# Weights loaded in runs of 128 columns, and four steps of a product moved, in a four-layer attention kernel

## The chip, the cores and the metric

The kernel runs on one core of a Trainium2 chip. A core has five engines that run side by side, each with its own queue of instructions: TensorE (PE in the profile; its weight loads are PEld) multiplies matrices, VectorE (DVE) and ScalarE (ACT) do elementwise work, GpSimd (POOL) does a little more of it, and SyncE (SP) issues DMA transfers. Sixteen DMA engines move the data between HBM and the core's memory (SBUF). The metric is device time in microseconds, the median of several executions. TensorE, VectorE and ScalarE hand data to each other through SBUF and through PSUM, the banks that matrix products are written to.

## What is computed

The input x has 8 images of 512 channels by 1024 positions. Four layers follow each other; what matters here is the first two, and of them the weights.

```python
# layer 0, per image b
f = relu(batchnorm(Wf @ x)); g = relu(batchnorm(Wg @ x)); h = Wh @ x      # 64 channels each
z = f.T @ g;  x = Wv @ (h @ (z / largest_singular_value(z)).T) + x
# layer 1
n = group_norm(x)
q = wq @ n + bq;  k = wk @ n + bk;  v = wv @ n + bv
x = x + wp @ (v @ softmax(q.T @ k / sqrt(512)).T) + bp
# layer 2: attention again with other weights; layer 3: a convolution with signs of weights and inputs
```

The statistics of layer 0's batchnorm run over all images, so all of x is read once before anything else can end.

The kernel doesn't compute q and k apart. With u = (wk.T wq) n the scores are u.T n, up to terms that the softmax drops, and with wo = wp wv the output projection is folded in too. So it makes two products of weights at the start, `wu` from q and k and `wo` from v and p, and two bias vectors: `bu`, the sum over the rows of wk weighted by bq, and `bo`, the sum over wp's columns weighted by bv (plus bp). Each of these is a sum over one common index of 512. Its order is free, so long as both factors have it in the same order.

## The kernel before, in words

**First passes (L1361 to L1413).** For b = 0 to 7, `load_x(b)` fetches an image in four DMAs of 512 KB (L141, the first image in five), one for each 128 channels, and TensorE multiplies it with the weights of f, g and h (L1376); for the last two images h is left for later. The tile `xt` has two buffers: the load of image b waits until pass b-2 has read its buffer for the last time. ScalarE and VectorE copy the products out and take statistics (L1395 to L1404). The last two images stay in their buffers.

**Loads between the images.** SP's queue is in program order. After the four x loads of b = 2, 3 and 4 it issues the loads of wq, wk and wv (`load_blocks`, L1334 to L1343), 16 DMAs of 64 KB each: a DMA fills 32 partitions, and its source is read in runs of 32 neighbouring columns. After v's come `load_rows` (L210 to L214): the bias row bg_row, the vector bvc (bv of layer 1) and Wv of layer 0 twice. Then come x of b = 5 and 6, the weights z, tpg and p (`load_w`, L156), and x of b = 7. A DMA instruction takes one of eight semaphores in turn, and waits until the DMA that had it before, eight DMAs earlier, has landed.

**Transposes.** In the product of weights, the common index has to lie on the partitions. The weights arrive with the other index there. `natural` (L1345 to L1350) turns each by four VectorE transposes of 32x32 blocks: with w on partitions 32 q to 32 q + 31 loaded from columns of group q, the transposed columns come to lie on those partitions. Which column is on which partition follows from the loads alone.

**Second part (L1551 to L1627).** TensorE's order is written out by hand: a generator `filler` yields after each small piece of independent work, and the main thread of work, which has dependent steps on other engines, takes so many steps of it (`next(todo)`) after each of its own. `filler` loads p, makes wu (`product`, L1420), the late h, the Gram matrices, the biases (`biases`, L1443 to L1468), and last wo, again by `product`: 16 matmuls of 512 columns, with a copy by ScalarE after each 8. The main thread is the chain for the largest singular value (`first_chain`) and then the entry of the first image into layer 1 (`entering(0)`, which runs `enter`, L421 to L467): the two products for the image's weights (L301), four visits with matmuls (L431) and VectorE work (L440 to L445), a mean (L452), a variance (L459), and small steps on VectorE and GpSimd that end in scale and bias. The list in L1622 says how many filler steps go behind each of the seven. Then the normalized h is made (L482), which the first product of u (L407, through `make_u`) waits for.

For the other engines a scheduler chooses the order; the memset of `ones2` (L1632), for instance, is one that it moves.

Of the kernel before, what the change touches and what calls it, by code (L numbers as in the profile page):

```python
# [8 lines left out]
F32 = mybir.dt.float32  # L9
# [7 lines left out]
P = 128  # L17
B = 8
C = 512
N = 1024  # L20
CC = C // P
# [4 lines left out]
MID = 64  # L26
# [34 lines left out]
COL = {n: 4 * i for i, n in enumerate(VEC512)}  # L61
# [9 lines left out]
QUAD = 32  # L71
# [16 lines left out]
def kernel(  # L88
# [17 lines left out]
    nc = tc.nc  # L106
    mm = nc.tensor.matmul

    const = ctx.enter_context(tc.tile_pool(name="const", bufs=1))
# [15 lines left out]
    def bank():  # L125
        return psum["bank"].tile([P, HF], F32, tag="bank", name="bank")
# [20 lines left out]
    def side(i):  # L147

        return slice(i * MID, (i + 1) * MID)


    sbw = {}

    def load_w(name, src, shape, pool=wpool, eng=nc.sync, tag=None):
        t = pool.tile(shape, F32, tag=tag or name, name=name)
        eng.dma_start(out=t, in_=src)  # L156
        sbw[name] = t
        return t
# [4 lines left out]
    a1 = early.enter_context(tc.tile_pool(name="a1", bufs=1))  # L163
# [38 lines left out]
    bg_row = const.tile([P, P], F32, tag="bg_row", name="bg_row")  # L202

    bvc = const.tile([P, CC], F32, tag="bvc", name="bvc")
    bhc = const.tile([P, 1], F32, tag="bhc", name="bhc")
    wv2 = const.tile([P, C], F32, tag="wv2", name="wv2")
    for i in range(2):
# [1 line left out]

    def load_rows():  # L210
        nc.sync.dma_start(out=bg_row, in_=rows[MID + C :].partition_broadcast(P))
        nc.sync.dma_start(out=bvc, in_=rows[MID : MID + C].rearrange("(cc p) -> p cc", p=P))
        for i in range(2):
            nc.sync.dma_start(out=wv2[side(i), :], in_=w_v0)  # L214

# [10 lines left out]
    def vec(name):  # L226
        return ct[:, COL[name] : COL[name] + CC]
# [1094 lines left out]
    def scale_z():  # L1322

        rep = a1.tile([P, CC, P], F32, tag="absw", name="rep")
        nc.vector.tensor_copy(rep, inv2.unsqueeze(2).to_broadcast([P, CC, P]))
        ps = bank()
        for oc in range(CC):
            mm(out=ps[:, bass.ts(oc, P)], lhsT=rep[:, oc, :], rhs=ident, start=True, stop=True)
        nc.vector.tensor_tensor(sbw["z"], sbw["z"], ps, ALU.mult)


    nat = {}

    def load_blocks(name, src, tag):  # L1334

        t = sbw[name] = a1.tile([P, 4, GROUPS, QUAD], F32, tag=tag, name="blocks_" + name)
        of = src.rearrange("(r a) c o -> r a (c o)", a=QUAD)
        for q in range(4):
            for r in range(4):
                nc.sync.dma_start(  # L1340
                    out=t[bass.ts(q, QUAD), r],
                    in_=of[r].rearrange("a (m w) -> a m w", w=P)[:, :, bass.ts(q, QUAD)],
                )  # L1343

    def natural(name, tag):  # L1345
# [16 lines left out]
    for b in range(B):  # L1362
# [3 lines left out]
        if b in (2, 3, 4):  # L1366
            load_blocks(*((("q", w_q, "q"), ("k", w_k, "k"), ("v", w_v, "v"))[b - 2]))
        if b == 4:
            load_rows()
# [45 lines left out]
    def product(lt, rhs, dst, vector):  # L1415
        for i in range(CC // 2):
            ps = wide()
            for k in range(2):
                for oc in range(CC):
                    one = mm(  # L1420
                        out=ps[:, half(k)],
                        lhsT=lt[:, oc, bass.ts(2 * i + k, P)],
                        rhs=rhs[:, oc, :],
                        start=oc == 0,
                        stop=oc == CC - 1,
                    )
                    if i + k + oc == 0:
                        tc.keep_in_program_order(one)
                    if k == 0 or oc < CC - 1:
                        yield  # L1430
            to = dst[:, 2 * i : 2 * i + 2, :].rearrange("p o c -> p (o c)")
            if i % 2 and vector:
                nc.vector.tensor_copy(to, ps)
            else:
                nc.scalar.copy(to, ps)
            yield

    def biases():

        part = a1.tile([P, 2, C], F32, tag="absw", name="part")
        for j, (w, v) in enumerate(((nat["k"], vec("L1_conv_bq")), (sbw["p"], bvc))):  # L1443
            t = part[:, j, :]
            for k in range(CC):
                if k == 0:
                    nc.vector.tensor_scalar(t, w[:, 0, :], v[:, 0:1], None, ALU.mult)
                else:
                    nc.vector.scalar_tensor_tensor(
                        t, w[:, k, :], v[:, k : k + 1], t, ALU.mult, ALU.add  # L1450
                    )
                yield False
        for j, dst in enumerate((bu, bo)):
            ps = bank()
            for i in range(CC):
                mm(
                    out=ps[:, i : i + 1],
                    lhsT=part[:, j, bass.ts(i, P)],
                    rhs=ones1,
                    start=True,  # L1460
                    stop=True,
                )
            if dst is bu:
                nc.vector.tensor_copy(bu, ps[:, 0:CC])
            else:
                nc.vector.tensor_tensor(bo, ps[:, 0:CC], vec("L1_conv_bp"), ALU.add)
            yield True
        nc.vector.tensor_tensor(bvo, bo, vec("L0_conv_bv"), ALU.add)  # L1468
# [82 lines left out]
    def filler():  # L1551

        load_w("p", w_p, [P, CC, C], a1, tag="v")
        yield from product(nat["q"], nat["k"], wu, True)
        for b in order[:2]:
            yield from late_h(b)
        yield from gram(jl, 2, ht_pair[jl], gtl)
        scale_z()  # L1560
        yield
        between = biases()
        sums = sums_u()
        for j in rest:
            for _ in grams(j):
                next(sums, None)
                yield
                if next(between, None):
                    yield
        yield from product(nat["v"], sbw["p"], wo, False)  # L1570

    todo = filler()
    with tc.manual_schedule(engines={mybir.EngineType.PE}):
        mv = a1.tile([P, 2, 2], F32, tag="mv", name="mv")
        mean = a1.tile([P, 2], F32, tag="mean", name="mean")
        dev = a1.tile([P, 2], F32, tag="dev", name="dev")
        for i in range(2):
            nc.vector.bn_aggr(mv[:, i, :], st[:, i, :, :])
        for _ in range(3):
            next(todo)  # L1580
        ps = bank()
        mm(out=ps[:, 0:2], lhsT=fold, rhs=mv[:, :, 0], start=True, stop=True)
        nc.vector.tensor_copy(mean, ps[:, 0:2])
        nc.vector.tensor_tensor(dev, mv[:, :, 0], mean, ALU.subtract)
        nc.vector.tensor_tensor(dev, dev, dev, ALU.mult)
        nc.vector.tensor_tensor(dev, dev, mv[:, :, 1], ALU.add)
        next(todo)
        ps = bank()
        mm(out=ps[:, 0:2], lhsT=fold, rhs=dev, start=True, stop=True)
        sc0 = rsqrt_eps(a1, ps[:, 0:2], 2, "r0")  # L1590
        bi0 = a1.tile([P, 2], F32, tag="bi0", name="bi0")
        m0 = a1.tile([P, 2], F32, tag="m0", name="m0")
        c0 = COL["L0_conv_bf"]
        bias, gamma, beta = (ct[:, c0 + 2 * i : c0 + 2 * i + 2] for i in range(3))
        nc.vector.tensor_tensor(sc0, sc0, gamma, ALU.mult)
        nc.vector.tensor_tensor(m0, mean, bias, ALU.add)
        nc.vector.tensor_tensor(bi0, bias, m0, ALU.subtract)
        nc.vector.tensor_tensor(bi0, bi0, sc0, ALU.mult)
        nc.vector.tensor_tensor(bi0, bi0, beta, ALU.add)
        jl = order[0] // 2  # L1600
        for i in range(2):
            for k in range(2):
                relu(2 * jl + k, i)
        for _ in range(5):
            next(todo)
        for ftl, gtl in turned_pair(jl):
            pass
        for i, t in ((0, ftl), (1, gtl)):
            for _ in gram(jl, i, t, t):
                next(todo)  # L1610

        relus = iter([(2 * j + k, i) for j in rest for i in range(2) for k in range(2)])

        steps = entering(0)
        for k, _ in enumerate(first_chain(jl)):

            for _ in range(4 if k == 3 * NSTEP + 3 else 2 if k % 3 == 1 or k == 0 else 1):
                next(todo, None)
            for args in (next(relus, None),):
                if args:  # L1620
                    relu(*args)
        for n in (2, 2, 2, 2, 4, 3, 6):  # L1622
            next(steps)
            for _ in range(n):
                next(todo, None)
        for _ in todo:
            pass  # L1627
# [194 lines left out]
```

## Time and profile before

| | |
|---|---|
| median of 3 runs | 1891.7 us (1891.26 to 1892.12) |
| the profiled execution's own time | 1891.29 us |
| its span, first to last instruction | 1889.5 us |
| TensorE busy | 1856.3 us, 98% |
| VectorE busy | 1122.5 us, 59% |
| ScalarE busy | 541.7 us, 29% |
| GpSimd busy | 121.8 us, 6% |
| the first passes over x, TensorE | 4.31 to 102.4 us |
| the first product of u begins | 191.11 us |
| DMA packets | 50114, of them 28848 under 512 B |

The span is what the profile shows, and the 1.8 us that the execution's time has more lie around it. A single precision matmul of 512 columns stands in the trace as two records. In a timeline each row is a run of like instructions: its start in us, its length, engine, line, operation, tiles, how many, and in brackets how long the engine sat idle before it, and what it waited for. Times in rows of SP (SPq) are those in which SP works at issuing a DMA, not those of the transfer. The chain of work that ended last is followed back from the last instruction of the program through whatever released each step.

### The profile page before, as it was taken

How to read it: one execution, taken by the hardware profiler on the slowest of the kernel's cores; microseconds unless marked ns; L12 is line 12 of the kernel's file. 1: busy time of each engine (PE TensorE's matmuls, PEld its weight loads, DVE VectorE, ACT ScalarE, POOL GpSimd, SP SyncE). 2: the span in 40 equal slices, each digit the busy share in tenths (PEclk: the TensorE clock that was granted, in tenths of full speed). 3: DMA queues.
4: the chain of work that ended last, by engine and by line, in shares of the span. 5: the costliest groups of instructions: out<-in, count | busy, mean ns of one | idle time of the engine just before them, and what ended most of it. 6: DMA issues, size and time to landing. Idle time of an engine off the chain costs nothing.

```text
span 1889.5 us, 16517 instructions
## 1 busy us (share of the span) xinstructions
PE 1856.3 (98%) x6196; PEld 949.7 (50%) x6196; DVE 1122.5 (59%) x2083; ACT 541.7 (29%) x882; POOL 121.8 (6%) x109
## 2 busy tenths in 40 slices
PE   8799999999999999999999999999999999999997
PEld 3246456544645456544645455544645455544653
DVE  3246686467774676467774676357653766355547
ACT  2032221145203521234203522144202521244114
POOL 1000000100020000200020001100020001100011
PEclk9999999999999999999999999999999999999999
DMA  8810000002000110002000110002000200000001
GB/s 247 259 57 7 1 6 12 1 12 89 18 1 1 53 54 12 1 12 89 18 0 1 62 44 12 1 30 71 12 0 12 89 12 1 1 34 23 12 0 47
DMA packets 50114, 66.52 MB, mean 35 GB/s; under 512 B 28848, under 2 KB 30060, under 8 KB 49772
## 3 DMA queue, kind: packets, MB, share of 16 engines
q1 hardware_dynamic: 49100, 64.96, 10.2%
q8 instruction: 51, 0.84, 0.2%
q10 hardware_dynamic: 864, 0.43, 0.1%
q14 instruction: 35, 0.29, 0.1%
q0 software_dynamic: 64, 0.00, 0.0%
HBM read 46.44 MB, written 18.94 MB: 35 GB/s over the span
## 4 chain that ended last, share of the span: by engine, by line
PE 93%; SPq 3%; DVE 2%; ACT 1%; DMA 1%; issue 0%; POOL 0%; DVEq 0%; ACTq 0%
PE bank L407 46%; PE bank L585 20%; PE bank L834 6%; PE bank L987 5%; PE bank L686 3%; PE bank L703 3%; SPq L1340 2%; PE bank L1376 2%; PE bank L431 2%; PE bank L726 1%; PE wide L1420 1%; PE bank L1478 1%; PE bank L1055 1%; PE bank L857 0%; PE quad L1268 0%
## 5 line engine op out<-in xcount | busy, mean ns | idle before, releaser
L585 PE MATMUL bank<-e,vt 128*128 128x512 f32 x768 | 336.2, 594 | 0.0
L585 PEld LDWEIGHTS bank<-e,vt 128*128 128x128 f32 x768 | 144.6, 190 | 172.1 <-issue 167.6
L407 PE MATMUL bank<-ut,h 128*128 128x512 f32 x384 | 178.9, 598 | 0.0
L407 PEld LDWEIGHTS bank<-ut,h 128*128 128x128 f32 x384 | 71.4, 190 | 94.5 <-issue 92.9
L407 PE MATMUL bank<-us,hs 128*128 128x512 f32 x256 | 115.6, 593 | 0.0
L834 PE MATMUL bank<-tpg 128*128 128x512 f32 x256 | 115.4, 596 | 0.0
L987 PE MATMUL bank<-e,tpg 128*128 128x512 f32 x256 | 114.7, 595 | 0.0
L358 DVE TENSOR_TENSOR e<-bank,e 128x512 f32<-128x512 f32 x96 | 66.2, 689 | 60.8 <-PE bank L407 50.6
L841 ACT ACTIVATE e<-bank 128x512 f32<-128x512 f32 x128 | 76.3, 597 | 67.0 <-PE bank L834 67.0
L407 PE MATMUL bank<-h,wu 128*128 128x512 f32 x192 | 91.7, 610 | 3.5 <-DVE h L482 3.5
L352 ACT COPY e<-bank 128x512 f32<-128x512 f32 x96 | 56.0, 584 | 118.9 <-PE bank L407 118.5
L407 PE MATMUL bank<-wo,h 128*128 128x256 f32 x384 | 89.9, 384 | 0.0
L238 POOL TENSOR_TENSOR r_r<-r_v,minus_half 128x4 f32<-128x4 f32 (+1 forms) x11 | 10.9, 988 | 1057.9 <-DVE r_v L237 1052.0
L987 PEld LDWEIGHTS bank<-e,tpg 128*128 128x128 f32 x256 | 48.2, 190 | 60.3 <-issue 59.9
L407 PEld LDWEIGHTS bank<-wo,h 128*128 128x128 f32 x384 | 71.5, 190 | 12.5 <-issue 3.8
L407 PEld LDWEIGHTS bank<-us,hs 128*128 128x128 f32 x256 | 48.5, 190 | 57.3 <-issue 54.4
L1376 PE MATMUL bank<-xt,fg 128*64 128x512 f32 x256 | 61.8, 627 | 15.7 <-DMA xt<-in_x 11.3
L846 DVE TENSOR_TENSOR esum<-esum,e 128x1024 f32<-128x1024 f32 x48 | 58.8, 1225 | 30.2 <-ACT e L841 29.9
L834 PEld LDWEIGHTS bank<-tpg 128*128 128x128 f32 x256 | 47.7, 191 | 54.9 <-issue 52.3
L714 ACT ACTIVATE sg<-xt,rb 128x512 f16<-128x512 f32 x64 | 44.2, 716 | 107.7 <-DVE xt L705 104.8
L358 DVE TENSOR_TENSOR vt<-bank,vt 128x512 f32<-128x512 f32 x48 | 33.2, 691 | 66.4 <-PE bank L407 65.6
L352 ACT COPY vt<-bank 128x512 f32<-128x512 f32 x64 | 37.3, 583 | 121.4 <-PE bank L407 121.3
(361 smaller groups left out, 2885.5 us busy)
## 6 DMA issues: line engine op xcount, KB each, us to landing
xt<-in_x SPq DMA_DIRECT2D x55, 512.0 KB
out<-both SPq DMA_DIRECT2D x63, 256.0 KB
rfull<-r_dram SPq DMA_DIRECT2D x15, 512.0 KB
f_dram<-f SPq DMA_DIRECT2D x8, 256.0 KB
fb<-f_dram SPq DMA_DIRECT2D x8, 256.0 KB
w<-in_w SPq DMA_DIRECT2D x1, 1024.0 KB
blocks_q<-in_w_q SPq DMA_DIRECT2D x16, 64.0 KB
blocks_k<-in_w_k SPq DMA_DIRECT2D x16, 64.0 KB
```

The source lines that it names most:

```text
L352: nc.scalar.copy(dst, ps)
L358: nc.vector.tensor_tensor(dst, ps, u, ALU.add)
L407: mm(out=ps[:, q * w : (q + 1) * w], lhsT=lt(ka, kb, q, k), rhs=rhs(ka, kb, q, k), start=first and q == 0 and k == 0, stop=last and k == 1 ...
L585: mm(out=ps, lhsT=a[:, t, bass.ts(r_, P)], rhs=e[t], start=first and t == 0, stop=last and t == NTH - 1, skip_group_check=True,)
L686: mm(out=ps[:, i, :], lhsT=xt[:, cc, bass.ts(4 * h + i, P)], rhs=sbw["tpg"][:, cc, 2 * P : 3 * P], start=cc == 0, stop=cc == CC - 1,)
L703: mm(out=ps, lhsT=sbw["z"][:, bass.ts(oc, P)], rhs=att, start=True, stop=True)
L714: nc.scalar.activation(sg[:, cc, :], xt[:, cc, half(h)], AF.Sign, bias=rb3[:, cc : cc + 1])
L834: mm(out=ps, lhsT=pt[:, 0, bass.ts(t, P)], rhs=tt[:, 0, half(h)], start=True, stop=True,)
L841: nc.scalar.activation(e[:, half(h)], ps, AF.Exp, scale=float(P) ** -0.5)
L846: nc.vector.tensor_tensor(esum, esum, e, ALU.add)
L987: mm(out=banks[h], lhsT=gt[:, t, :], rhs=es[t][:, half(h)], start=t == 0, stop=t == NT - 1,)
L1376: mm(out=banks[i][side(h), :], lhsT=w0[i][:, cc, :], rhs=xt[:, cc, half(h)], start=cc == 0, stop=cc == CC - 1,)
```

## The change

Four things change.

1. `load_blocks` reads runs of 128 neighbouring columns where it read runs of 32. The number of DMAs (16 for each weight), their size (64 KB) and their 32 partitions stay; a group q of 32 partitions now gets columns 128 q to 128 q + 127 of each row chunk, where it got columns 32 q to 32 q + 31 out of each 128. The transposes are not touched. Through them the common index comes in another order on partitions and chunks.
2. p has to have its rows in that same order, and is loaded in four DMAs of 256 KB, one for each group of 32 partitions, where it was one of 1 MB with 128 partitions.
3. The two vectors that weight the rows in `biases` need that order too. bvc is loaded in four DMAs of 32 partitions by 4 elements, where it was one of 128 by 4. bq was read from the tile of all columns that is there anyway; a tile of its own, bqc, is now loaded by four more DMAs. These are all on SP's queue, in `load_rows`.
4. The list of filler steps is (2, 2, 2, 2, 3, 2, 4) where it was (2, 2, 2, 2, 4, 3, 6).

```diff
@@ -202,6 +202,7 @@
     bvc = const.tile([P, CC], F32, tag="bvc", name="bvc")
+    bqc = const.tile([P, CC], F32, tag="bqc", name="bqc")
@@ -209,7 +210,11 @@
     def load_rows():
         nc.sync.dma_start(out=bg_row, in_=rows[MID + C :].partition_broadcast(P))
-        nc.sync.dma_start(out=bvc, in_=rows[MID : MID + C].rearrange("(cc p) -> p cc", p=P))
+        rv = rows[MID : MID + C].rearrange("(q m b) -> q b m", q=4, b=QUAD)
+        rq = cols.rearrange("(m b) n -> n b m", b=QUAD)
+        for q in range(4):
+            nc.sync.dma_start(out=bvc[bass.ts(q, QUAD), :], in_=rv[q])
+            nc.sync.dma_start(out=bqc[bass.ts(q, QUAD), :], in_=rq[COL["L1_conv_bq"] + q])
         for i in range(2):
             nc.sync.dma_start(out=wv2[side(i), :], in_=w_v0)
@@ -1334,12 +1339,12 @@
         t = sbw[name] = a1.tile([P, 4, GROUPS, QUAD], F32, tag=tag, name="blocks_" + name)
-        of = src.rearrange("(r a) c o -> r a (c o)", a=QUAD)
+        of = src.rearrange("(r a) c o -> r a c o", a=QUAD)
         for q in range(4):
             for r in range(4):
                 nc.sync.dma_start(
-                    out=t[bass.ts(q, QUAD), r],
-                    in_=of[r].rearrange("a (m w) -> a m w", w=P)[:, :, bass.ts(q, QUAD)],
+                    out=t[bass.ts(q, QUAD), r].rearrange("a (c m) b -> a c (m b)", c=CC),
+                    in_=of[r][:, :, bass.ts(q, P)],
                 )
@@ -1440,7 +1445,7 @@
-        for j, (w, v) in enumerate(((nat["k"], vec("L1_conv_bq")), (sbw["p"], bvc))):
+        for j, (w, v) in enumerate(((nat["k"], bqc), (sbw["p"], bvc))):
@@ -1552,7 +1557,10 @@
-        load_w("p", w_p, [P, CC, C], a1, tag="v")
+        t = sbw["p"] = a1.tile([P, CC, C], F32, tag="v", name="p")
+        of = w_p.rearrange("(m b) c o -> c b m o", b=QUAD)
+        for q in range(4):
+            nc.sync.dma_start(out=t[bass.ts(q, QUAD)], in_=of[q])
         yield from product(nat["q"], nat["k"], wu, True)
@@ -1619,7 +1627,7 @@
-        for n in (2, 2, 2, 2, 4, 3, 6):
+        for n in (2, 2, 2, 2, 3, 2, 4):
             next(steps)
             for _ in range(n):
                 next(todo, None)
```

In the order of the instructions that follows from it, TensorE's differs only around the entry: of the last matmuls of wo there are 3 before the mean (L452), 2 before the variance (L459) and 2 behind it, where there were 4, 3 and none. On VectorE one instruction moves, the memset of ones2: from before the variance's steps (L237) to directly ahead of L482. ScalarE and GpSimd keep their order. SP's queue has the same order with ten more DMAs, and p's first DMA is where p's one was, ahead of x of b = 7, the other three behind it.

## The prediction

> **What bounds the kernel now.** I read the engine shares first, then the chain of work that ended last, then SP's and TensorE's timelines where the chain leaves TensorE. The chain, by line:
>
> ```profile
> PE bank L407 46%; PE bank L585 20%; PE bank L834 6%; PE bank L987 5%; PE bank L686 3%; PE bank L703 3%; SPq L1340 2%; PE bank L1376 2%; PE bank L431 2%; PE bank L726 1%; PE wide L1420 1%; PE bank L1478 1%; PE bank L1055 1%; PE bank L857 0%; PE quad L1268 0%
> ```
>
> TensorE carries 93% of it. The foreign entry is SPq L1340, SP issuing the block loads: 2.2% of 1889.5 us, some 41.6 us. SP's timeline there (start, length, then the group):
>
> ```profile
> 17.43 1.76 SPq L141 DMA_DIRECT2D xt<-in_x  x4
> 19.23 14.58 SPq L1340 DMA_DIRECT2D blocks_q<-in_w_q  x16
> 33.92 1.98 SPq L141 DMA_DIRECT2D xt<-in_x  x4
> 35.94 13.39 SPq L1340 DMA_DIRECT2D blocks_k<-in_w_k  x16
> 49.44 2.08 SPq L141 DMA_DIRECT2D xt<-in_x  x4
> 51.56 14.89 SPq L1340 DMA_DIRECT2D blocks_v<-in_w_v  x16
> 66.50 0.62 SPq L211 DMA_DIRECT2D bg_row<-in_rows  x1
> 67.16 0.43 SPq L212 DMA_DIRECT2D bvc<-in_rows  x1
> 67.63 1.48 SPq L214 DMA_DIRECT2D wv<-in_w_v  x2
> 69.22 4.44 SPq L141 DMA_DIRECT2D xt<-in_x  x8
> ```
>
> SP never rests from 17.43 to 73.7. The x of b=3, 4, 5 may be fetched when pass b-2 has released its buffer (28.4, 39.5 and 51.4 us on TensorE's timeline), but is issued at 33.92, 49.44 and 69.22: 5.5, 9.9 and 17.8 us late. TensorE pays:
>
> ```profile
> 53.92 2.25 PE L1376 MATMUL bank<-xt,fg 128*64 128x512 f32 x8 [2.49 <-DMA xt<-in_x]
> 56.65 1.08 PE L1376 MATMUL bank<-xt,fg 128*64 128x512 f32 x4 [0.49 <-DMA xt<-in_x]
> 58.77 4.51 PE L1376 MATMUL bank<-xt,fg 128*64 128x512 f32 x20 [1.03 <-DMA xt<-in_x]
> ...
> 74.08 8.60 PE L1376 MATMUL bank<-xt,fg 128*64 128x512 f32 x32 [6.63 <-DMA xt<-in_x]
> ```
>
> An undisturbed pass is b=2, 28.27 to 39.30: 11.03 us. Pass 3 (39.30 to 51.29) is 0.96 over, pass 4 (to 67.31) 4.99, pass 5 (to 86.72) 8.38: **14.3 us lost**. That is more than the 11.3 us of marked waits, because after 6.63 us of rest 32 records take 8.60 instead of 7.09 us. It is not the DMA engines that are short (columns: stretch, busy us of PE, PEld, DVE, ACT, POOL, PE clock, DMA share, GB/s):
>
> ```profile
> 60.00:65.00 5.00, 5.00 (x26) 1.76 (x24) 2.37 (x4) 0.48 (x1) 0.00 (x0) 1.00 0.53 82
> ...
> 80.00:85.00 5.00, 5.00 (x28) 1.74 (x26) 2.50 (x4) 0.00 (x0) 0.00 (x0) 1.00 1.04 417
> ```
>
> With blocks alone they are half busy at 82 GB/s; with x they reach 417. The second place is the entry into the first u:
>
> ```profile
> 184.48 0.31 PE L452 MATMUL bank<-mv,gmat 128*128 128x4 f32 x2
> 184.65 2.82 PE L1420 MATMUL wide<-p,nat_v 128*128 128x512 f32 x6
> 187.31 0.28 PE L459 MATMUL bank<-dev,gmat 128*128 128x4 f32 x2
> 191.11 9.84 PE L407 MATMUL bank<-h,wu 128*128 128x512 f32 x16 [3.52 <-DVE h L482]
> ```
>
> TensorE reaches L459 only at 187.31 though DVE finished dev at 185.58, and then rests 3.52 us until the chain L459, L237, L238 to L482 gives h.
>
> [...]
>
> **Block loads.** In steady state a block DMA (512 runs) takes SP 0.626 us, 0.67 from start to start; some stall behind x to 3.5 us, so the mean is 42.9/48 = 0.89. The new one has 128 runs of 512 B, a form that the trace has: fg's four loads (128 x 512 B) take 0.41 to 0.46 us; x (128 x 4 KB) takes 0.43. Against it stands bg_row, 128 x 512 B in 0.62 us, directly behind the blocks, where x too is slow (0.55). I take 0.45, 0.495 from start to start; bounds 0.40 and 0.67.
>
> By the landing records, x's first chunk lands 3.6 us after issue with nothing ahead and the next three 1.3 us apart; a small DMA lands after 2.5 us. SP keeps eight DMAs in flight: each issue waits for the one eight before. So, with x of b=2 landing from 21.1 on as before, q's fifth to eighth wait for its chunks, the ninth goes at 25.4, and x of b=3 at 25.4 + 8 x 0.495 = 29.4, landed by 36.9, wanted at 39.3. k's fifth to eighth wait for those chunks, the ninth goes at 37.5, x of b=4 at 41.5, landed by 49.0, wanted at 50.3. v's ninth goes at 49.6.
>
> **Vectors.** bvc's one DMA becomes four, and four for bqc are added: 7 more on SP ahead of b=5's x, each of 128 elements of 4 B. bvc with 512 took 0.43; I take 0.495 again, 3.5 us in all. x of b=5 goes after v's last 8 and 11 row loads: 49.6 + 19 x 0.495 = 59.0. Its chunks land at 62.6, 63.9, 65.2, 66.5; pass 5 could use them at 61.4, 62.2, 63.1, 64.0. **2.5 us of wait remain**[...]. x of b=6 lands by 71.4, wanted at 76; b=7's goes when pass 5 ends and lands in pass 6, as now. So what is late next, once the blocks are quicker, is b=5's x alone. Front: 14.3 - 2.5 = **11.8 us** gained.
>
> **p.** One DMA becomes four over 32 partitions, the first behind tpg as now, three behind b=7's x, so about 1.5 us more on SP where the next issue, f_dram, waits for ReLU anyway. p lands near 85 us, DVE wants it (L1447) near 133: nothing, and that cover is 48 us. Transposes, products and bias sums have the same instructions in the same order, over permuted rows: nothing. Their data come earlier than now (v's last block near 55 us, its transposes behind g's statistics of b=4 near 60), so DVE's queue gets no new wait; bvc and bqc are read first near 133 us.
>
> **Four steps.** L1420's last matmuls go 4, 3, 0 around L452 and L459 before, 3, 2, 2 after. L452 stays: mv is ready at 184.36. L459 has two matmuls ahead instead of three, 0.86 us earlier; h follows. The two left run 186.6 to 188.4, inside the rest that ends at 190.3. Scalar's copy of wo then ends at 189.5; L407 waits for Scalar here, 0.8 us of cover. The memset of ones2 (0.17 us) moves directly ahead of L482, between dependent steps: 0.05. **0.8 us** gained (bounds: 0.86 if the memset hides wholly, -0.2 if it is paid in full and the earlier L459 brings nothing).
>
> Sum against the profiled execution's 1891.29 us: -11.8 - 0.8 = 1878.7; the median, 1891.7, lies 0.4 higher, so 1879.0. After 190 us TensorE is the chain, and the rest shifts as a whole.
>
> **Rivals.**
> - The blocks issue at x's best pace or the vectors are cheaper, x of b=5 goes by 56.5 and nothing is left to wait: 1891.7 - 14.3 - 0.8 = 1876.6. For: bare issues of 0.33 in the trace. Against: 27 DMAs behind each other, 0.43 in a row. Chance 0.15.
> - The issue falls little, 0.60 from start to start, as bg_row hints: b=5's x at 61.9, 5.5 us of wait and up to 1 of slow clock: 1882 to 1883. Chance 0.18.
> - Slower: SP's time goes by the DMA, not by the runs, so blocks stay at 0.89 and seven more vector loads push b=5's x back 3.5 us; less 0.8 from the entry: 1894.4. It decides when blocks average over 0.86: from 19.23 SP needs 42.9 for blocks, 4.1 for x and 2.7 for rows now; rows become 5.4 to 6.2, and the entry pays 0.8. For: bvc's 512 elements took no longer than x's 128. Against: fg's 0.45. Chance 0.05.
> - Nothing: the x transfers, not their issue, are late. Against: 23.4 MB at 417 GB/s need 56 of 95 us. 1891.7, chance 0.03.
> - Mine: 0.59, its own range 1877.5 to 1881.
>
> The first three kinds of gain hold 0.92; 1875.5 to 1883.5 covers them and the price bounds. About 0.2% (3.8 us) is what a measurement of this kernel can tell from no change. Faster 0.92, same 0.03, slower 0.05.
>
> **What would show it.** L1340's groups near 0.45 us each; x of b=3 and b=4 issued near 29.4 and 41.5 without waits in passes 3 and 4; b=5's near 59 with about 2.5 us of DMA waits; L1420 beginning near 90.6 instead of 102.39; a clock of 1.0 in 70 to 80; L459 to L407 3.8 us as now, with two L1420 between. Wrong if L1340's mean stays above 0.6, if the 4 B loads land late enough to hold the eighth issue after them, or if L407 waits for the copy of wo.

## The result, and where the time went

The changed kernel takes 1888.72 us (median of 18 runs, 1887.60 to 1890.78), the kernel before 1892.34 us on the same chip (18 runs, 1891.26 to 1895.09). The ratio is 0.998, with an interval of 0.9973 to 0.9987: 2.5 to 5.1 us faster. The forecast was 1879.0 us, its range 1875.5 to 1883.5. The kernel became faster, but by little more than a quarter of what was expected. The profiled executions are 1889.26 us (span 1887.4) after and 1891.29 (span 1889.5) before.

The chain of the changed kernel, by line. The functions lie five lines lower than before, so L412 is what L407 was, L1345 is the block load, L1381 the first passes and L1425 the product of weights:

```profile
PE bank L412 46%; PE bank L590 20%; PE bank L992 6%; PE bank L839 6%; PE bank L691 3%; PE bank L708 3%; PE bank L1381 2%; DMA xt<-in_x 2%; PE bank L436 1%; PE bank L731 1%; PE wide L1425 1%; SPq L1345 1%; PE bank L1060 1%; PE bank L1483 1%;
```

The foreign entry SPq has halved to 1%, and beside it stands a new one, the transfers of x, with 2%. The way into layer 1 is still led by loads; only the name of what holds them has changed. SP's timeline (start, length, group):

```profile
17.05 1.75 SPq L141 DMA_DIRECT2D xt<-in_x  x4
18.85 13.51 SPq L1345 DMA_DIRECT2D blocks_q<-in_w_q  x16
32.47 1.95 SPq L141 DMA_DIRECT2D xt<-in_x  x4
34.46 13.11 SPq L1345 DMA_DIRECT2D blocks_k<-in_w_k  x16
47.67 2.13 SPq L141 DMA_DIRECT2D xt<-in_x  x4
49.85 14.50 SPq L1345 DMA_DIRECT2D blocks_v<-in_w_v  x16
64.39 0.59 SPq L212 DMA_DIRECT2D bg_row<-in_rows  x1
65.02 0.43 SPq L216 DMA_DIRECT2D bvc<-in_rows  x1
...
69.12 1.17 SPq L219 DMA_DIRECT2D wv<-in_w_v  x2
70.39 4.51 SPq L141 DMA_DIRECT2D xt<-in_x  x8
```

The x of b = 3 and 4 goes 1.45 and 1.77 us earlier than before, the x of b = 5 goes 1.17 us **later** (70.39, was 69.22). That a group of 16 has hardly become shorter hides two things that a tile's own view separates. First the kernel before, q's blocks: shortest, median and longest issue in ns.

```profile
L1340 SPq DMA_DIRECT2D blocks_q<-in_w_q x16: 624/626/3503, 19.2 to 33.2; - x16
```

And the kernel after:

```profile
L1345 SPq DMA_DIRECT2D blocks_q<-in_w_q x16: 560/597/735, 18.9 to 31.8; - x16
```

The median fell only from 626 to 597 ns. The long issues, up to 3.5 us, are gone (the longest of all 48 is now 1.13 us): over all 48 block DMAs SP worked 40.9 us before and 29.4 us after. What replaced them is in SP's own waits (what it waited for: us in all, times, the longest). Before, from 15 to 75 us, no block load waits:

```profile
SPq L141 <- PE bank L1376: 6.6, 1, 6.6
SPq L156 <- DMA xt<-in_x: 0.3, 1, 0.3
```

After, the same stretch:

```profile
SPq L1345 <- DMA xt<-in_x: 9.9, 7, 2.5
```

So 11.4 us less issuing was answered by 9.9 us of new waits for x's landings. Before, SP sat in a long issue behind each image's transfer until about 26.5 us; after, it runs on, has eight DMAs in flight, and stands until x's last chunk has landed at 26.65, the same moment: q's eighth block, the eighth DMA behind that chunk, waits 2.54 us and goes at 26.66. In the chain of the changed kernel that landing stands as a piece of its own (start, length), from the issue of x's last chunk on:

```profile
18.38 8.27 DMA xt<-in_x
```

For b = 3 and 4 the pieces are 7.88 and 8.73 us long.

The account of b=5's x, by the starts in the two timelines: the whole begins 0.38 us earlier, q's part is 1.07 shorter, k's 0.32, and v's up to bg_row 0.34. From bg_row to x it takes 6.00 us instead of 2.72, 3.28 longer for seven more DMAs. Together that makes the 1.17 us later.

TensorE's timeline, the passes over b = 4 and 5 and the start of the product of weights:

```profile
51.84 1.08 PE L1381 MATMUL bank<-xt,fg 128*64 128x512 f32 x4 [1.66 <-DMA xt<-in_x]
53.29 1.08 PE L1381 MATMUL bank<-xt,fg 128*64 128x512 f32 x4 [0.37 <-DMA xt<-in_x]
55.12 1.08 PE L1381 MATMUL bank<-xt,fg 128*64 128x512 f32 x4 [0.75 <-DMA xt<-in_x]
58.15 6.21 PE L1381 MATMUL bank<-xt,fg 128*64 128x512 f32 x20 [1.95 <-DMA xt<-in_x]
...
74.55 9.57 PE L1381 MATMUL bank<-xt,fg 128*64 128x512 f32 x32 [6.02 <-DMA xt<-in_x]
...
103.83 1.55 PE L1425 MATMUL wide<-nat_k,nat_q 128*128 128x512 f32 x3
```

Pass 4 (50.06 to 68.41) is 7.3 us over an undisturbed 11.03, pass 5 (68.41 to 88.16) another 8.7: 16.0 us lost where it was 14.3. The product of weights begins at 103.83, was 102.39. Nothing is gained at the front. The 1.4 us by themselves say little: among profiled executions with the same loads the product begins at 102.58 and 105.75 (in two of the runs below), and with the loads of before it begins at 103.29 in another.

The DMA engines did get what the change gives them (busy us of PE, PEld, DVE, ACT, POOL, PE clock, DMA share, GB/s):

```profile
60.00:65.00 5.00, 5.00 (x22) 1.62 (x20) 1.18 (x2) 0.00 (x0) 0.00 (x0) 0.75 0.33 92
```

A third busy at 92 GB/s where it was 0.53 at 82. But in this stretch nobody waited for them: TensorE is busy for all of its 5.00 us, and SP waits for no landing.

All of the gain is at the other end, at the entry into the first u:

```profile
185.84 0.39 PE L457 MATMUL bank<-mv,gmat 128*128 128x4 f32 x2 [0.61 <-DVE mv L456]
186.09 1.96 PE L1425 MATMUL wide<-p,nat_v 128*128 128x512 f32 x4
187.88 0.28 PE L464 MATMUL bank<-dev,gmat 128*128 128x4 f32 x2
188.03 1.96 PE L1425 MATMUL wide<-p,nat_v 128*128 128x512 f32 x4
191.69 7.11 PE L412 MATMUL bank<-h,wu 128*128 128x512 f32 x16 [1.71 <-DVE h L487]
```

From the beginning of the product of weights to the first u it takes 87.86 us, was 88.72: 0.86 earlier. And the first 16 records of u take 7.11 us, were 9.84: 2.73 less, because the clock is 1.00 from 190 to 200 us where it was 0.50 and then 0.84. The first of these stretches, before and after (the clock is the third number from the end):

```profile
190.00:195.00 5.00, 3.89 (x5) 1.85 (x6) 4.82 (x11) 0.10 (x1) 0.00 (x0) 0.50 0.01 3
190.00:195.00 5.00, 3.31 (x8) 1.63 (x9) 4.86 (x15) 1.60 (x2) 0.00 (x0) 1.00 0.02 3
```

0.86 and 2.73 gain 3.6 us, the later front takes 1.4 back; that is the 2.1 us between the two spans, within 0.1.

### The profile page after: what moved, and what is told of

Its sections match the earlier page's. It is cut to its first block, busy times and chain, and to the rows that moved or that the text cites. A ratio compares the mean times of both kernels' runs of the same rounds, so it can differ in the third digit from the quotient of the medians.

```text
span 1887.4 us, 16534 instructions
## 1 busy us (share of the span) xinstructions
PE 1855.8 (98%) x6196; PEld 948.2 (50%) x6196; DVE 1121.6 (59%) x2083; ACT 542.0 (29%) x882; POOL 121.9 (6%) x109
## 3 DMA queue, kind: packets, MB, share of 16 engines
q1 hardware_dynamic: 31724, 64.96, 10.3%
## 4 chain that ended last, share of the span: by engine, by line
PE 94%; DMA 2%; DVE 2%; SPq 1%; ACT 1%; issue 0%; POOL 0%; ACTq 0%; DVEq 0%
PE bank L412 46%; PE bank L590 20%; PE bank L992 6%; PE bank L839 6%; PE bank L691 3%; PE bank L708 3%; PE bank L1381 2%; DMA xt<-in_x 2%; PE bank L436 1%; PE bank L731 1%; PE wide L1425 1%; SPq L1345 1%; PE bank L1060 1%; PE bank L1483 1%; PE bank L862 0%
## 5 line engine op out<-in xcount | busy, mean ns | idle before, releaser
L412 PE MATMUL bank<-ut,h 128*128 128x512 f32 x384 | 178.9, 597 | 0.0
L412 PEld LDWEIGHTS bank<-ut,h 128*128 128x128 f32 x384 | 71.3, 190 | 94.7 <-issue 93.0
L412 PE MATMUL bank<-us,hs 128*128 128x512 f32 x256 | 115.6, 593 | 0.0
L412 PE MATMUL bank<-h,wu 128*128 128x512 f32 x192 | 89.0, 594 | 1.7 <-DVE h L487 1.7
L412 PE MATMUL bank<-wo,h 128*128 128x256 f32 x384 | 89.9, 384 | 0.0
L1381 PE MATMUL bank<-xt,fg 128*64 128x512 f32 x256 | 63.7, 644 | 15.3 <-DMA xt<-in_x 10.7
L412 PEld LDWEIGHTS bank<-wo,h 128*128 128x128 f32 x384 | 71.4, 190 | 12.6 <-issue 3.8
L412 PEld LDWEIGHTS bank<-us,hs 128*128 128x128 f32 x256 | 48.4, 190 | 57.5 <-issue 54.5
```

The source lines that it names most:

```text
L412: mm(out=ps[:, q * w : (q + 1) * w], lhsT=lt(ka, kb, q, k), rhs=rhs(ka, kb, q, k), start=first and q == 0 and k == 0, stop=last and k == 1 ...
L1381: mm(out=banks[i][side(h), :], lhsT=w0[i][:, cc, :], rhs=xt[:, cc, half(h)], start=cc == 0, stop=cc == CC - 1,)
```

## The experiments

Each ran beside the kernel before on the same chip, and each ratio is to that. Where no interval is given, there is one time and its profile.

### Each half alone

The first run is the kernel before with only the list changed.

```diff
-        for n in (2, 2, 2, 2, 4, 3, 6):
+        for n in (2, 2, 2, 2, 3, 2, 4):
```

> The kernel before with the new list of steps alone. Theory A (clock): two matmuls behind L459 shorten TensorE's rest before the first u from 3.5 us to some 1.7, so the clock stays whole; 0.9 us from the earlier variance and some 2.7 us from the first 16 records of u (7.1 instead of 9.8 us): 3.6 us faster than before, near 1888.7, the whole gain of the change. Rival B (chain only): 0.9 us faster, near 1891.4, and the rest of the gain comes from the loads.

Measured: 1888.34 us (21 runs), 0.9986 (0.9979 to 0.9992), 1.5 to 4.0 us faster. Its timeline at the entry:

```profile
187.48 1.96 PE L1420 MATMUL wide<-p,nat_v 128*128 128x512 f32 x4
191.13 7.11 PE L407 MATMUL bank<-h,wu 128*128 128x512 f32 x16 [1.70 <-DVE h L482]
```

The rest of 3.52 us has been cut to 1.70 by the matmuls left over, and the clock stays up, 1.00 from 190 to 200 us: 7.11 us instead of 9.84. The waits for x are those of before (2.54, 0.36 and 6.88 us). One line of the list gives the time of the whole change.

The second run is the changed kernel with the old list, the same line the other way round.

> The changed kernel with the old list of steps: the loads alone. Theory A: the loads gain nothing, the first passes end 0 to 1.5 us later than before, u starts cold: 1892.3 to 1893.8. Rival B: the loads gain 2.7 us, near 1889.6.

Measured: 1892.22 us (13 runs), 1.0002 (0.9994 to 1.0011).

```profile
191.28 8.80 PE L412 MATMUL bank<-h,wu 128*128 128x512 f32 x16 [3.52 <-DVE h L487]
```

The loads alone, with their vectors, are worth nothing that can be measured. The 3.52 us rest is back, and with it a slow start of u; here it costs 1.7 us, not 2.7. (The profiled execution took 1890.44 us, 1.8 under the median.)

How short must the rest be? The third run is the changed kernel with only one piece left over, not two.

```diff
-        for n in (2, 2, 2, 2, 3, 2, 4):
+        for n in (2, 2, 2, 2, 4, 2, 4):
```

> The changed kernel with 4, 2, 1 matmuls around the mean and the variance instead of 3, 2, 2: the variance as early as in the changed kernel, one matmul behind it, and TensorE's last rest before u 2.6 us instead of 1.7. Theory A (clock by the length of the rest): 2.6 us is still short enough, the first 16 records of u take 7.1 us, the time is the changed kernel's, 1888.7. Rival A2 (any longer rest costs in proportion): half of the 2.7 us comes back, near 1890.

Measured: 1889.51 us (13 runs), 0.9988 (0.998 to 0.9997).

```profile
193.61 8.80 PE L412 MATMUL bank<-h,wu 128*128 128x512 f32 x16 [2.56 <-DVE h L487]
```

In this execution a rest of 2.56 us costs 1.69 of the 2.73 us, so the expectation that 2.6 us is short enough fell. But it is the slowest of the 13 (1892.90 us, the median is 1889.51), and the times do not tell this kernel from the changed one: the intervals overlap. Its four slowest executions have a mean granted clock of 0.994, the nine others 0.995 to 0.996, so the clock need not have fallen here in all of them.

A trace records the granted clock itself. Up to the program's end the slow stretches are 6.83 and 6.83 us long in the kernel before, 3.41 and 6.83 in the changed one, and the full ones between them 112.64 and 10.24 us, all within 0.01 us of multiples of 3.413. Lay a grid of this step over each of the two traces so that it meets them, and add up TensorE's idle time in every cell of the grid that is at full clock (from the clock's first record on, at 8.88 and 7.92 us, and the program's end left out). Four cells were followed by half the clock: they hold 2.87 and 2.19 us of rest before, 3.41 and 1.95 after. Of the others none has more than 1.83 us. So the length of a single rest did not decide: the kernel before has one of 2.49 us ahead of pass 4 that lies in two cells, 1.8 us of it in the first, and the clock stayed full, while the changed kernel's 1.95 us lie in one and half the clock followed. The changed kernel's rest of 1.71 us ahead of u is shorter than all four by itself, wherever it lies. For two other runs there is the clock by windows, from 190 to 195 and from 195 to 200 us: 0.66 and 1.00 in the run with the old list, 0.94 and 0.72 in this third one, which is 3.4 us at half in each (1.7 us lost). In the kernel before it was 6.83 us, of which u had 5.5 (2.7 lost). That is a reading of the traces; no run was made to test it.

### Fewer DMAs

If SP's time goes by the DMA, a quarter of them should free it. Here each weight comes in 4 DMAs of 256 KB; the rows are split the other way, so that one partition holds four neighbouring rows, and the transposes write to match.

```diff
-        of = src.rearrange("(r a) c o -> r a c o", a=QUAD)
+        of = src.rearrange("(a r) c o -> a (r c) o", a=QUAD)
...
-            for r in range(4):
-                nc.sync.dma_start(
-                    out=t[bass.ts(q, QUAD), r].rearrange("a (c m) b -> a c (m b)", c=CC),
-                    in_=of[r][:, :, bass.ts(q, P)],
-                )
+            nc.sync.dma_start(
+                out=t[bass.ts(q, QUAD)].rearrange("a r (c m) b -> a (r c) (m b)", c=CC),
+                in_=of[:, :, bass.ts(q, P)],
+            )
...
-        to = t.rearrange("p o (c r a) -> p r c o a", r=4, a=QUAD)
+        to = t.rearrange("p o (c a r) -> p r c o a", r=4, a=QUAD)
```

> The changed kernel with the four DMAs of a group of 32 partitions merged into one of 256 KB, 4 per weight instead of 16, the runs still 512 B (rows split the other way round, put right in the transposes' output). Theory C (number of DMAs): SP pays some 0.6 us a DMA whatever its runs, so a weight costs SP 3 us instead of 13 to 14.5, x of b = 3, 4, 5 is issued when its buffer is free, and of the 16 us that passes 4 and 5 lose some 15 are regained: near 1874, first passes done near 89 us. Rival D (transfer): 32 partitions in runs of 512 B take in their 1 MB at some 90 GB/s however they are issued, 11 us a weight, and x waits behind them: 1885 to 1889.

Measured: 1875.67 us (4 runs), 0.9916 (0.99 to 0.9931). SP's timeline:

```profile
19.93 3.71 SPq L1344 DMA_DIRECT2D blocks_q<-in_w_q  x4
29.18 1.76 SPq L141 DMA_DIRECT2D xt<-in_x  x4
30.98 4.17 SPq L1344 DMA_DIRECT2D blocks_k<-in_w_k  x4
40.21 1.76 SPq L141 DMA_DIRECT2D xt<-in_x  x4
42.02 5.08 SPq L1344 DMA_DIRECT2D blocks_v<-in_w_v  x4
...
58.25 5.85 SPq L141 DMA_DIRECT2D xt<-in_x  x8
```

Four DMAs take SP 3.7 to 5.1 us where sixteen took 13 to 14.5. The x of b = 3 and 4 now goes when its buffer is released (SP waits for TensorE there, 19.4 us in four waits, not for a landing), and the passes have no wait but four of 0.2 us in pass 5; the product of weights begins at 90.52. The transposes take 1.13 us where they took 0.67. Only their output differs, now with a stride of 16 B. No matmul waits for them. This is the gain that the forecast had sought, and theory C's time within 2 us. Merging takes away both hindrances at once, the issues and the waits for x: four DMAs of x and four of a weight make eight in flight, and from 15 to 66 us no block waits for x to land (9.9 us in the changed kernel). How much is due to each, this run does not tell.

To see what the longer runs add to it, the same merging was tried on the kernel before: runs of 32 columns, 2048 runs in each DMA, old list.

```diff
-        of = src.rearrange("(r a) c o -> r a (c o)", a=QUAD)
+        of = src.rearrange("(a r) c (m w) -> a (r c m) w", a=QUAD, w=P)
...
+            nc.sync.dma_start(
+                out=t[bass.ts(q, QUAD)].rearrange("a r g b -> a (r g) b"),
+                in_=of[:, :, bass.ts(q, QUAD)],
+            )
...
```

The lines left out take away the old loads and turn the transposes' output as in the run before.

> The kernel before with the four DMAs of a group merged into one of 256 KB, with its own runs of 32 columns (2048 runs of 128 B a DMA), old list of steps, old vectors and p. Theory C (number of DMAs): SP is free as in the merged changed kernel; 14.3 us of lost passes become 1 to 4, 1878 to 1881. Rival G (128 B runs are what holds SP and x[...]): SP stalls behind each merged DMA[...], x waits as now: 1886 to 1891.

Measured: 1882.94 us (4 runs), 0.9952 (0.9937 to 0.9967), between the two theories.

```profile
L1339 SPq DMA_DIRECT2D blocks_q<-in_w_q x4: 742/1546/6482, 20.1 to 28.6; - x4
```

One issue stalls for 6.5 us: with 2048 short runs in a DMA, SP is held in the issue itself; by what, was not shown. x of b = 5 goes at 61.84 and pass 5 waits 4.40 and 0.41 us. With the new list, worth 2.6 us by the ratio of the first run, this kernel would stand near 1880.3, some 4.7 us above the merged one with long runs. That is an estimate, and rather too small, since the merged changed kernel also carries seven more vector loads. The run length does count, then, when the DMAs are few; with sixteen for each weight, the loads with longer runs gained nothing that can be measured.

### The vectors

The changed kernel with its eight vector loads moved behind x of b = 6.

```diff
+        for i in range(2):
+            nc.sync.dma_start(out=wv2[side(i), :], in_=w_v0)
+
+    def load_vectors():
...
-        for i in range(2):
-            nc.sync.dma_start(out=wv2[side(i), :], in_=w_v0)
...
+        if b == 6:
+            load_vectors()
```

> The changed kernel with the eight DMAs for bvc and bqc behind x of b = 6 instead of ahead of b = 5. Theory C: x of b = 5 is issued some 4 us earlier, its wait of 6.0 us falls by as much and the clock's penalty after it shrinks too: 4 to 5.5 us faster than the changed kernel, near 1884. Rival D (x of b = 5 is held by transfers ahead of it, not by SP): 1888 to 1889.

Measured: 1884.79 us (6 runs), 0.9965 (0.9953 to 0.9977); the medians lie 3.9 us apart, the ratios 2.8. SP's and then TensorE's timeline:

```profile
63.48 0.59 SPq L212 DMA_DIRECT2D bg_row<-in_rows  x1
64.12 1.17 SPq L214 DMA_DIRECT2D wv<-in_w_v  x2
65.82 4.60 SPq L141 DMA_DIRECT2D xt<-in_x  x8
```

```profile
71.02 8.58 PE L1385 MATMUL bank<-xt,fg 128*64 128x512 f32 x32 [4.97 <-DMA xt<-in_x]
```

x of b = 5 goes 4.57 us earlier. Of that, 3.66 are the loads moved away, from bg_row to x (2.34 us, was 6.00); the rest arose before bg_row, where the two kernels are alike. Pass 5 begins 3.53 us earlier, and its first 32 records take 8.58 us, not 9.57. Its wait fell only from 6.02 to 4.97 us, because pass 4 ended 2.5 us earlier here too. In the changed kernel the small loads gave back what the blocks had gained.

### What form of DMA costs SP how much

These three have the changed kernel's number of DMAs, their size and its list, and load other columns or partitions than the reference needs, so that their products of weights are other numbers; they measure the loads. First, one run of 2 KB per partition:

```diff
-                    out=t[bass.ts(q, QUAD), r].rearrange("a (c m) b -> a c (m b)", c=CC),
-                    in_=of[r][:, :, bass.ts(q, P)],
+                    out=t[bass.ts(q, QUAD), r].rearrange("a g b -> a (g b)"),
+                    in_=of[r][:, q, :],
```

> The changed kernel with each block DMA still 64 KB on 32 partitions, but one run of 2 KB a partition (32 runs instead of 128). It reads other columns than wanted, so the products of weights are of other numbers; the work is the same. Theory C (SP pays by the DMA): SP's steady step stays near 0.60 us. Rival E (SP pays by the run, from 128 on): it falls to x's 0.43 or below, each weight costs SP 2.5 us less and x of b = 5 is issued some 7 us earlier.

Measured: 1884.66 us. An issue takes 0.420 us in steady state, x of b = 5 goes at 63.49, so theory C, 0.60 whatever the form, fell. But SP waits 12.3 us for x's landings within the blocks.

Second, 128 partitions with one run of 512 B each, the form of fg's loads from which the forecast took its price:

```diff
-                    out=t[bass.ts(q, QUAD), r].rearrange("a (c m) b -> a c (m b)", c=CC),
-                    in_=of[r][:, :, bass.ts(q, P)],
+                    out=t[:, r, bass.ts(q, 4)].rearrange("p g b -> p (g b)"),
+                    in_=src[:, r, bass.ts(q, P)],
```

> The changed kernel with each block DMA 64 KB on 128 partitions, one run of 512 B each, 16 a weight as before (the columns come to other partitions than wanted, so the products of weights are of other numbers; the work is the same). This is the form of fg's loads, which the forecast took its 0.45 us from. Theory C (by the DMA, whatever the form): 0.60 us. Rival F (the number of partitions or the two-level pattern costs): 0.43 to 0.46 us, a weight 2.3 us cheaper on SP.

Measured: 1879.12 us. The tile's view, and SP's waits from 15 to 66 us:

```profile
L1344 SPq DMA_DIRECT2D blocks_q<-in_w_q x16: 328/430/625, 18.8 to 29.5; - x16
```

```profile
SPq L1344 <- DMA xt<-in_x: 9.0, 8, 2.0
```

x of b = 5 goes at 61.01, pass 5 waits 3.91 us. With the form that the forecast had priced, its price comes out. That the time is the forecast's 1879.0 too is luck: the product of weights begins at 93.75, 8.6 us earlier than before and not 11.8, and the entry gains 3.6 us and not 0.8.

Third, the source of the first of these (2 KB that lie together) written to four places of 512 B in each partition:

```diff
-                    out=t[bass.ts(q, QUAD), r].rearrange("a (c m) b -> a c (m b)", c=CC),
-                    in_=of[r][:, :, bass.ts(q, P)],
+                    out=t[bass.ts(q, QUAD), :, bass.ts(r, 4)].rearrange("a i g b -> a i (g b)"),
+                    in_=of[r][:, q, :].rearrange("a (i w) -> a i w", w=P),
```

> The changed kernel's block DMAs read the 2 KB that lie together in a row of the weight (as the run with 2 KB per partition did, issue 0.420 us), but write them to four places of 512 B in each partition; the columns are others, so the weights' products aren't the reference's. If SP's time follows from several runs in a partition, the issue is back at 0.60 us, x of b = 5 goes near 70 and the time is near 1888 to 1889. If it follows from a source that is scattered (runs 2 KB and more apart in HBM), the issue stays near 0.42, x of b = 5 goes near 62 and the time is near 1880 to 1884.

Measured: 1885.18 us.

```profile
L1345 SPq DMA_DIRECT2D blocks_q<-in_w_q x16: 312/430/710, 19.8 to 31.1; - x16
```

```profile
SPq L1345 <- DMA xt<-in_x: 13.0, 8, 2.6
```

Several places on the SBUF side do not make the issue dear: 0.430 us, not 0.60. What is left is several runs per partition on the HBM side, 2 KB apart in the changed kernel. But bvc, with four elements per partition that lie 128 B apart in HBM, took 0.43 too, so a rule for 0.43 and 0.60 is not shown, and stays open. One candidate was not tried by itself: the blocks' source is a pattern of three levels (row, chunk, run), bvc's of two.

The time was missed (1880 to 1884 expected), and that is the more useful finding. The second and the third run spend the same on issuing, 21.5 and 21.6 us over the 48, but the third waits 13.0 us for x's landings and the second 9.0, and x of b = 5 goes at 66.08 instead of 61.01 (1.0 of it is a later beginning, 18.01 instead of 17.00). Cheap issues are a part only; when x's last chunk lands behind the blocks is the other: 9.4 to 10.3 us after x's first issue in the third run, 8.0 to 8.8 in the second. Why 128 partitions hold x up less than 32 was not tried.

### Both at once

The merged loads with the vectors behind x of b = 6, the two edits shown above.

> The changed kernel with both edits at once: each weight in 4 DMAs of 256 KB, and the eight vector loads behind x of b = 6 instead of ahead of x of b = 5. With the merged loads alone 1875.67 us was measured, x of b = 5 was issued at 58.25 and pass 5 kept four waits of about 0.2 us. If x of b = 5 is still a little late there, moving some 3.5 us of issues behind it takes these waits away: 1874.5 to 1875.2. Rival: the passes are bound by TensorE already, and the time stays at 1875.7 within 0.5; then pass 5 lasts 11 us in both.

Measured: 1874.14 us (4 runs, 1873.56 to 1876.38), 0.9908 (0.9892 to 0.9925). SP's and TensorE's timeline:

```profile
51.77 10.79 SPq L141 DMA_DIRECT2D xt<-in_x  x8
```

```profile
49.56 7.04 PE L1384 MATMUL bank<-xt,fg 128*64 128x512 f32 x32
...
60.60 7.04 PE L1384 MATMUL bank<-xt,fg 128*64 128x512 f32 x32
...
87.56 2.84 PE L1428 MATMUL wide<-nat_k,nat_q 128*128 128x512 f32 x6
```

The passes have no wait left; pass 4 lasts 11.04 us and pass 5 11.13. It is the fastest of these kernels, 18 us below the kernel before. That it beats the merged loads alone is seen in the trace (the four waits of 0.2 us are gone) but not settled by the times, whose intervals overlap.

## Why the prediction was wrong

**What bounds the kernel** was right. The late x cost the 14.3 us that the prediction had read: the last kernel takes them all away and is 18 us faster, of which the steps at the entry are 3.6. One reading in it falls short: the 14.3 us are 3.0 more than the marked waits, and the slow records that it gives as the reason explain 1.5. Much of the rest lies at the breaks: four records by themselves take 1.08 us, in a row of 32 (7.04 us) 0.88.

**Block loads: the step that failed**, in two of its terms. The first is the price, "I take 0.45, 0.495 from start to start". It measured 0.597 and 0.643, and the sign that the prediction had named for being wrong, a mean above 0.6, came: 29.4/48 = 0.61. The price came from fg's loads, with the same number of runs of the same length, but over 128 partitions with one run each, and issued by ScalarE at the start; the new blocks have 32 partitions with four. The run with 128 partitions shows that form at 0.43 on SP, and the changed kernel its own at 0.60. The prediction had set bg_row's 0.62 against it, and that was the right number for a wrong reason: bg_row takes 0.59 behind the changed blocks and 0.43 behind the cheap ones, so its length went with the DMA in front of it.

The second term is x's landing: "the next three 1.3 us apart", so landed 7.5 us after issue and the ninth block 0.5 after that. Measured, the last chunks of b = 2, 3 and 4 land 9.6, 9.4 and 10.4 us after the first issue, and by the last of the form experiments the blocks behind them have a part in it. The trace of before has nearly the same (9.2, 8.8 and 9.3 us in the landing records), so it could have been read there. The two together explain the whole of b=5's x at 70.39 instead of 59.0:

| | us |
|---|---|
| ninth block against x's first issue: 10.22, 10.01 and 11.06, predicted 7.97, 8.1 and 8.1 | 7.1 later |
| from the ninth of q and k to the next x: 5.20 and 5.19, predicted 4.0 | 2.4 later |
| from v's ninth to x of b = 5: 11.66, predicted 9.4 | 2.3 later |
| x of b = 2 begins 0.38 earlier than before | -0.4 |

So the larger of the two terms was the landing, some 7 of the 11.4 us, not the price. That is also why the rival with 0.60 from start to start and 1882 to 1883 us fell: it corrected the price alone.

**The waits left**, 2.5 us, follow from that: the passes 4 and 5 lost 16.0 us. Nor did the waits cost their own length alone: behind the last of pass 4's, 1.95 us, the clock was at half for 3.41 us.

**Vectors**: right in kind and in size, 3.5 us predicted, 3.28 us more between bg_row and x. Moving them gave 2.8 to 3.9 us back. The rival that ended slower rested on these, and put its turning point at blocks of 0.86 us on the average. Its own figures give 0.84 to 0.85 (42.9 us less 2.7 to 3.5 for the vectors, plus 0.8 from the entry, over 48). By SP's groups, waits within them counted, the blocks came to 41.1/48 = 0.857, so it was close to what happened at the front: x of b = 5 went later, and with the old list the time is that of before. The entry's 3.6 us, which it had at 0.8, kept the change on the faster side.

**p, the transposes, products and biases**: nothing, as predicted; p lands between 88 and 101 us, not near 85, and is first read at 146.2.

**Four steps**: right in its mechanism, with one term missing. L464 is reached 0.87 us and L412 0.86 earlier as worked out, the memset is hidden (0.31 us between the two dependent steps around it, was 0.30), and L457 stays though TensorE now rests 0.61 before it. But the prediction had slower records after a rest in its own text (8.60 us for 32 after 6.63 us, not 7.09), and the 9.84 us of the first 16 records in its fence, and asked only what the shorter rest saves, not what it does to the clock behind it. That is 2.73 us against 0.86. The term of 0.8 measured 3.6 in the profile, and 1.5 to 4.0 us in the run with the list alone. Of the sum, then, 11.8 us at the front came to nothing, and 0.8 at the entry to 3.6. (The sum itself is 0.1 off: 1891.7 less 12.6 is 1879.1.)

## What to carry to other kernels

Before pricing a DMA by another one in the trace, compare the partitions and the runs per partition on both sides, not only bytes and count; and when an issue gets cheaper, ask which landing the queue runs into next (11.4 us less issuing met 9.9 us of new waits here), reading the landing times from the trace rather than spacing them evenly. If SP never rests and the DMA engines are half idle, try fewer DMAs first: here a quarter of them took the changed kernel from 1888.72 us to 1875.67, where the longer runs alone measured 1892.22, no gain. A short piece of independent work put into a rest of TensorE can be worth more than the rest that it fills, by what the clock would have lost afterwards: here the rest became 1.8 us shorter, and the 16 records behind it took 2.73 us less.

## What was not expected of the hardware

- A DMA of 64 KB took SP 0.626 us in 512 runs of 128 B, 0.597 us in 128 runs of 512 B with four on a partition, 0.430 us in 128 runs on 128 partitions and 0.420 us in 32 runs of 2 KB. One of 256 KB with 512 runs of 512 B took some 0.7 us where nothing held it up: the issue hardly goes by the bytes.
- A DMA of many runs held SP in its issue at times: up to 3.5 us at 512 runs of 128 B behind x, 6.5 us at 2048.
- The clock fell after rests well under 3.41 us, the step of its slow stretches: in the traces of before and after, the four steps that half the clock followed hold 1.95 to 3.41 us of rest, the others at full clock 1.83 at most. In pass 4 of the changed kernel, behind a rest of 1.95 us, 20 records took 6.21 us; in the kernel before, behind one of 1.03, they took 4.51.
